# A graph layer on one core: SyncE fetches two sets of 128 edges row by row in chunks away from the stores of packs, and one beside them

## The chip, the core and the metric

The kernel runs on one core of a Trainium2 chip. A core has TensorE (PE: matrix products), VectorE (DVE), ScalarE (ACT), GpSimd (POOL) and SyncE (SP); each runs its own queue of instructions in order, and semaphores tie the queues together. SyncE computes nothing here: it issues transfers. ScalarE and SyncE issue transfers whose addresses are written in the instruction or held in a register; POOL issues indirect gathers, for which 128 row numbers lie in memory. The metric is the device time of one execution in microseconds (us), less is better.

## The reference

One layer of a graph network over 50000 nodes with 160 features each and 1650000 directed edges, sorted by their target, every node with an edge to itself among them. For each edge the source's features are combined with the edge's four numbers by five small weight matrices; the results are summed over the edges of each target, passed through two more matrices, and the layer ends with residuals and a norm:

```python
ss, vv = (s[src], v[src])
e0 = sh[:, 0:1]
e1 = sh[:, 1:4]
dot = jnp.einsum('eui,ei->eu', vv, e1)
out0 = C0 * (ss * e0 @ W1 + dot * INV3 @ W2)
...
m_agg = jax.ops.segment_sum(m, dst, num_segments=n)
...
return x + jax.nn.relu(h)
...
x = _layernorm(x + _L0_gnn_ref(x, edge_attr_4, L0_gnn_W1, L0_gnn_W2, L0_gnn_W3, L0_gnn_W4, L0_gnn_W5, L0_gnn_Ws, L0_gnn_Wv, edge_index), axis=-1)
```

Everything between the gather and the relu is linear in the source's features. So the kernel first sums, for each node, the source rows weighted by each of the four edge numbers, and multiplies by the (merged) weights once per node.

## The kernel before

**Sets, groups, pairs, chunks.** The edges come in *sets* of 128. For one set, 128 rows of `x` (640 bytes each) lie on the 128 partitions, and one product on PE sums them: the left operand `ha` holds, for each edge, its four numbers at the column of its target. Twelve sets are a *pair* of groups, the unit `p` of the main loop; ten pairs are a *chunk* of 120 sets, for which the edge list is loaded and turned at once. There are 105 chunks, numbered from 0. `gather` (L465) says where a set's rows come from: as a rule POOL fetches all 128 by one indirect gather into a tile `xg` (L473), of which there are four, each for a pair. PE waits for each set on its semaphore in `group_sums` (L517, the product at L522). Then VectorE turns the sums (L537) and adds them to a ring of node sums (L546), PE multiplies finished blocks by the weights (L841), VectorE forms residual and norm, and SyncE sends the result (L939).

**Fetchers.** Some sets are not gathered by POOL: another engine fetches their 128 rows one at a time, each with a transfer of 640 bytes whose address is in a register. A `Fetcher` does that, one for ScalarE (tiles `xscalar`) and one for SyncE (`xsync`). `spots(s)` says at which places among the 120 of chunk `s` they stand. `list_rows` (L403) has VectorE turn the row numbers of these sets into byte offsets (`held`, `line`, L412 and L413). From these the engine loads 32 offsets at a time into registers (L377) and issues one transfer for each (L381). `begin` and `deal` pace them: the rows of chunk `s` are dealt out evenly over ten pairs, from pair 4 of chunk `s - 1` to pair 4 of chunk `s`, between whatever else the engine issues.

```python
n = self.counts[s % len(self.counts)] if self.first <= s < NSC - 1 else 0
ats = [math.ceil((FBEGIN + per * (i + 1) / n + FWAIT - per) * PG * G) + self.place for i in range(n)]
```

ScalarE fetches three sets and two sets by turns, from chunk 6 on; SyncE one a chunk, at place 104, from chunk 8 on.

**Packs.** From chunk 5 on the kernel reads an edge list that it has compacted itself: edges from a node to itself are taken out and kept apart (`selves`). That is done in eleven *packs* of up to 128 rows of 1185 edges. A pack's steps, on VectorE mostly, are spread over some nine chunks by due times worked out from when its edges are needed (`due`); near their end SyncE writes the pack back by 17 steps of `store` (L734, each up to 16 transfers at L758), and `read` loads the next one (L615 to L619).

**What sets the order.** The order of each engine's queue is the order in which the program writes the instructions: in the main loop (L1021 to L1073), after each of a pair's twelve products, come a piece of node work, the rows of the fetchers that are due, and the pack's steps that are due. SyncE's queue also carries the loads of edges (`r`, `fd`), of nodes (`xt`, `xr`, `sa`), and the results.

Of the kernel before, what the change touches and what calls it, by code (L numbers as in the profile page):

```python
# [46 lines left out]
ET = mybir.EngineType  # L47
# [31 lines left out]
REST = 15  # L79
LEAD = 3  # L80
BY_SCALAR, SCALAR_FIRST = (3, 2), 6
BY_SYNC, SYNC_FIRST = (1,), 8
FBEGIN, FWAIT = 4, 4

def plan(n_nodes, n_edges):
# [24 lines left out]
def tile_gnn_resnorm(ctx: ExitStack, tc: tile.TileContext, x, src, dst, attr, W1, W2, W3, W4, W5, Ws, Wv, out, n_edges):  # L110
# [110 lines left out]
    NSC = math.ceil(NG / SG)  # L221
# [12 lines left out]
    with tc.tile_pool(name="once", bufs=1) as once, tc.tile_pool(name="raw", bufs=2) as rawp, \  # L234
# [23 lines left out]
        per = SG // PG  # L258
# [42 lines left out]
        def cast(loaded):  # L301
            s, at, ri, fi, fd, ef, af = loaded
            if ri is not None:
                ef = rawp.tile([P, 2, NK, W], F32, name="rf")
                fd = rawp.tile([P, 1], F32, name="ff")
                if s:
                    nc.scalar.copy(fd, fi)
                    begun.append(nc.scalar.copy(ef, ri))
                else:
                    begun.append(nc.vector.tensor_copy(ef[:, 0], ri[:, 0]))  # L310
                    soon.append((ef, ri, fd, fi))
            return s, at, fd, ef, af
# [34 lines left out]
                                                        skip_runtime_bounds_check_because="held within bounds")  # L347
            return spot_of.pop(g)

        fetched = {}  # L350

        class Fetcher:

# [3 lines left out]
                self.landed = [tc.alloc_semaphore(f"{pool.name}{i}") for i in range(4 * (max(counts) + 1))]  # L357

            def spots(self, s):
                n = self.counts[s % len(self.counts)] if self.first <= s < NSC - 1 else 0  # L360
                ats = [math.ceil((FBEGIN + per * (i + 1) / n + FWAIT - per) * PG * G) + self.place for i in range(n)]
                assert all(0 <= at < per * PG * G for at in ats)
                return ats
# [422 lines left out]
        def begin_segment(k):  # L786

            ring[k] = ringp.tile([P, ND, TW], F32, name="ring")
            own = own_blocks(k)
            end = min((own[-1][-1] + 1) * P, nblocks * P) - k * S if own else 0  # L790
            nc.vector.memset(ring[k][:, :, end:], 0.0)
# [61 lines left out]
        steps = place(cast(load(0)))  # L853
# [124 lines left out]
        START = 2  # L978
# [14 lines left out]
        packs, due = [], []  # L993
# [7 lines left out]
        reads, packs = [read for read, _ in packs], [steps for _, steps in packs]  # L1001
        packs[0][:0] = [reads[0], None, None, None]
        done, began = 0, START

        begin_segment(0)
        for k in range(1, NSEG):
            p = first_of[k] // PG
# [5 lines left out]
        for b, g in enumerate(last_of):  # L1013
            p = g // PG
# [79 lines left out]
    with tc.tile_pool(name="up", bufs=1) as up, tc.tile_pool(name="us", bufs=2) as us, tc.For_i(0, once_more, 1):  # L1094
# [18 lines left out]
        for s in range(nseg):  # L1113
# [7 lines left out]
            for c in range(CB):  # L1121
# [3 lines left out]
                at = us.tile([PB, 2, SEG], F32, name="at")  # L1125
# [18 lines left out]
    with tc.tile_pool(name="edges2", bufs=2) as ep, tc.tile_pool(name="ops2", bufs=2) as op, \  # L1144
            tc.tile_pool(name="node2", bufs=1) as np_, tc.tile_pool(name="psA2", bufs=2, space=PSUM) as psA, \
            tc.tile_pool(name="psF2", bufs=1, space=PSUM) as psF:
        with tc.For_i(0, blocks, 1) as b:
# [35 lines left out]
            for h in range(2):  # L1183
# [3 lines left out]
                at = np_.tile([D // 2, NK, NBLK], F32, name=f"ac{h}")  # L1187
# [3 lines left out]
            i = 0  # L1191
# [44 lines left out]
```

## Time and profile before

| what | value |
|---|---|
| median of 3 runs | 15331.41 us (15308.89 to 15333.12) |
| the profiled execution's own time | 15340.96 us |
| its span, from the first to the last instruction | 15339.1 us |
| granted clock of TensorE, mean | 0.583 |
| sets gathered by POOL | 12181 |
| sets fetched by ScalarE, by SyncE | 245 (31360 rows), 96 (12288 rows) |

Rows of the profile name the line, the engine and the operation, the tile written and the ones read, a count, and then times: in groups of instructions the busy us, the mean ns of one, and after the bar the idle time of the engine just before them with what ended it. `PEld` is the load of PE's left operand; `SPq` and `ACTq` are transfers issued by SyncE and ScalarE; a releaser called "issue" means that the engine waited for nothing the profile shows. PE shows two records for a product in 32-bit floats.

### The profile page before, as it was taken

The numbers are of one execution on the slowest core, as the hardware profiler recorded it, in microseconds if no ns is written. First come the engines' busy times: TensorE is split into PE (matmuls) and PEld (weight loads), VectorE is DVE, ScalarE is ACT, GpSimd is POOL, SyncE is SP. The second block draws the span as 40 slices with busy tenths as digits, with TensorE's granted clock in tenths as the row PEclk, the third lists the DMA queues.
The fourth block names the chain that finished last, engine by engine and source line by source line (L and its number), as shares of the span: only waits on it lengthen the run. The fifth ranks groups of instructions, "written<-read, shape, count | busy, mean of one in ns | idle before, by whom it ended". The sixth has DMA issues, their size and how long they took to land. (4 is left out here: it accounts for less than half of the span.)

```text
span 15339.1 us, 182899 instructions
## 1 busy us (share of the span) xinstructions
PE 9998.2 (65%) x28971; PEld 6683.8 (44%) x28972; DVE 7656.0 (50%) x12665; ACT 171.7 (1%) x273; POOL 11588.2 (76%) x12194
## 2 busy tenths in 40 slices
PE   3666566666666666666666666666666666666666
PEld 3444344444444444444444444444444444444444
DVE  8455365445635543563465355445634553554333
ACT  0000000000000000000000000000000000000000
POOL 7777777777777777777777777777777777777777
PEclk6555655555556555555555555555555555655555
DMA  3333333333333333333333333333333333333333
GB/s 82 99 82 93 90 84 86 96 90 83 92 90 87 84 95 91 82 86 95 91 83 92 89 87 84 96 90 82 86 98 89 81 88 88 87 86 86 85 82 74
DMA packets 916668, 1347.44 MB, mean 88 GB/s; under 512 B 296782, under 2 KB 691138, under 8 KB 912806
## 3 DMA queue, kind: packets, MB, share of 16 engines
q0 software_dynamic: 584688, 998.65, 28.1%
q1 hardware_dynamic: 266794, 315.98, 6.7%
q10 hardware_dynamic: 63984, 21.08, 0.8%
q14 instruction: 971, 7.95, 0.2%
q8 instruction: 231, 3.78, 0.1%
HBM read 1263.28 MB, written 71.42 MB: 87 GB/s over the span
## 5 line engine op out<-in xcount | busy, mean ns | idle before, releaser
L473 POOL DMA_INDIRECT xg<-in_x,si x12181 | 11584.7, 951 | 3722.2 <-issue 3591.6
L522 PE MATMUL ps<-xg,ha 128*128 128x160 f32 x24362 | 9236.8, 496 | 5305.4 <-DMA xg<-in_x,si 4585.4
L522 PEld LDWEIGHTS ps<-xg,ha 128*128 128x128 f32 x24362 | 5688.8, 289 | 8616.2 <-DMA xg<-in_x,si 7920.1
L537 DVE STREAM_TRANSPOSE sums<-ps 128x320 f32<-128x320 f32 x1044 | 535.1, 513 | 6130.6 <-PE ps L522 6089.1
L497 DVE TENSOR_TENSOR ha<-hot,pk 128x1536 f32<-128x1536 f32 x1044 | 1830.3, 1753 | 35.9
L841 PE MATMUL phb<-BWk,ring 128*128 128x160 f32 (+1 forms) x3910 | 1250.5, 417 | 0.0
L841 PEld LDWEIGHTS phb<-BWk,ring 128*128 128x128 f32 (+1 forms) x3910 | 1023.7, 295 | 0.0
L546 DVE TENSOR_TENSOR ring<-ring,sums 128x160 f32 x2087 | 684.3, 328 | 325.1 <-issue 190.1
L494 DVE TENSOR_TENSOR hot<-bank,rel 128x384 f32<-128x384 f32 x1044 | 573.1, 549 | 11.2 <-DMA xt<-in_x 9.4
L707 DVE COPY_PREDICATED prow<-marks,prow 128x2370 f32<-128x2370 int32 (+5 forms) x198 | 548.7, 2771 | 1.1
L832 DVE STREAM_TRANSPOSE ring<-xr 128x1280 f32<-128x1280 f32 x188 | 467.8, 2488 | 6.5
L707 DVE COPY_PREDICATED pra<-marks,pra 128x1580 f32<-128x1580 int32 (+5 forms) x198 | 377.0, 1904 | 0.0
L828 DVE TENSOR_TENSOR xr<-xr,bank 128x1280 f32<-128x1280 f32 x188 | 278.9, 1483 | 6.8 <-DVE bank L827 0.5
L186 DVE SCALAR_TENSOR_TENSOR y<-phb,xt 128x320 f32<-128x320 f32 x196 | 95.5, 487 | 296.7 <-PE phb L841 296.2
L826 DVE TENSOR_TENSOR sa<-sa,bank 128x32 f32<-128x32 f32 x188 | 29.7, 158 | 381.7 <-DMA sa<-selves 381.7
L196 ACT ACTIVATE rstd<-mv,eps_t 128x2 f32<-128x2 f32 x196 | 58.0, 296 | 13960.1 <-DVE mv L191 7936.4
L522 PE MATMUL ps<-xscalar,ha 128*128 128x160 f32 x490 | 168.8, 445 | 0.0
L543 DVE TENSOR_TENSOR ring<-ring 128x196 f32<-128x196 f32 (+20 forms) x485 | 149.1, 373 | 1.8
L644 DVE TENSOR_TENSOR hit<-marks,prow 128x395 f32<-128x395 f32 (+1 forms) x33 | 28.0, 847 | 242.4 <-ACT marks L643 242.4
L522 PEld LDWEIGHTS ps<-xscalar,ha 128*128 128x128 f32 x490 | 137.2, 314 | 0.0
L202 DVE TENSOR_SCALAR o<-y,mv,rstd 128x160 f32<-128x160 f32 x391 | 132.3, 380 | 7.5
L704 DVE COPY_PREDICATED_SCALAR hit<-marks,none 128x395 int32 (+5 forms) x198 | 129.7, 655 | 7.0
(352 smaller groups left out, 2369.6 us busy)
## 6 DMA issues: line engine op xcount, KB each, us to landing
xscalar<-in_x ACTq DMA_DIRECT2D x31360, 0.6 KB
xsync<-in_x SPq DMA_DIRECT2D x12288, 0.6 KB
xg<-in_x,si POOLq DMA_INDIRECT x12181
xr<-in_x SPq DMA_DIRECT2D x187, 640.0 KB
r<-edges SPq DMA_DIRECT2D x100, 384.0 KB
edges<-prow SPq DMA_DIRECT2D x1330, 27.8 KB
xt<-in_x SPq DMA_DIRECT2D x195, 160.0 KB
out<-o SPq DMA_DIRECT2D x195, 160.0 KB
```

The lines of the kernel that those rows point to most:

```text
L202: nc.vector.tensor_scalar(o[:n, i], y[:n, i], mv[:n, i, 0:1], rstd[:n, i:i + 1], op0=ALU.subtract, op1=ALU.mult)
L473: part = nc.gpsimd.indirect_dma_start(out=xg[:, j, :], out_offset=None, in_=x, in_offset=bass.IndirectOffsetOnAxis(ap=placed[0][:, u + j:u ...
L494: idle[:] = [nc.vector.tensor_tensor(hot[:, :n], slotsP[:, 0:W].unsqueeze(1).to_broadcast([P, n, W]), rel[:, u:u + n].unsqueeze(2).to_broa ...
L497: nc.vector.tensor_tensor(ha[:, :n], hot[:, :n].unsqueeze(2).to_broadcast([P, n, NK, W]), pk[:, :, u:u + n].rearrange("p k u -> p u k").un ...
L522: mm = nc.tensor.matmul(ps[:, j // G, :], ha[:, j].rearrange("p k w -> p (k w)"), xr, start=j % G == 0, stop=j % G == G - 1)
L537: nc.vector.transpose(at[:, :ng], ps[:, :ng].rearrange("p g (b f) -> p g b f", f=FB))
L543: nc.vector.tensor_tensor(ring[k][:, b, :past], ring[k][:, b, :past], ring[k - 1][:, b, S:S + past], op=ALU.add)
L546: nc.vector.tensor_tensor(here, here, at[:, i], op=ALU.add)
L707: nc.vector.copy_predicated(what[:n, a:e], mi[:, r].unsqueeze(2).to_broadcast([n, e - a, what.shape[2]]), what[:n, a + d:e + d])
L828: nc.vector.tensor_tensor(xr[:, :nq], xr[:, :nq], sumP[:, :nq].unsqueeze(2).to_broadcast([P, nq, D]), op=ALU.mult)
L832: nc.vector.transpose(ring[k][:, :, c0:c0 + nq * W].rearrange("p b (w q) -> p q b w", q=nq), xr[:, :nq].rearrange("p q (b f) -> p q b f", ...
L841: wrote("misc", nc.tensor.matmul(ph[:nb], ring[k][:, i, c0:c0 + nb], BWk[:, i, :], start=i == 0, stop=i == ND - 1))
```

## The change

SyncE's fetcher gets two counts, two and one. Which one holds in a chunk is no longer its number's turn but a question: does a store of a pack stand within the ten pairs in which the chunk's rows are dealt out, or in the ten before? If so, one set, else two. For that the places of all stores are worked out ahead of the main loop, from the packs' steps and due times. The fetcher also gets one more tile (three rather than two) and twelve semaphores rather than eight, since both are sized by the larger count; `line` and `held` become one place wider. ScalarE's fetcher is as before.

```diff
-BY_SYNC, SYNC_FIRST = (1,), 8
+BY_SYNC, SYNC_FIRST = (2, 1), 8
...
-        fetched = {}
+        fetched, stores = {}, []
+
+        def storing(s):
+
+            p = (s - 1) * per + FBEGIN
+            return any(p - per <= at < p + per for at in stores)
...
             def spots(self, s):
-                n = self.counts[s % len(self.counts)] if self.first <= s < NSC - 1 else 0
+                turn = s if self.et != ET.SP else storing(s)
+                n = self.counts[int(turn) % len(self.counts)] if self.first <= s < NSC - 1 else 0
...
+        for steps, a, b in zip(packs, [START] + due, due):
+            stores += [a + (i + 1) / len(steps) * max(1, b - a) for i, step in enumerate(steps)
+                       if isinstance(step, partial) and step.func.__name__ == "store"]
```

Lines after the change are numbered 6 higher from the fetcher on (9 from the main loop on). Of the 96 chunks from number 8 to 103, 56 get two sets and 40 one, in stretches: 8 and 9 two, 10 to 13 one, 14 to 18 two, 19 to 22 one, and so on to 100 to 103 with two.

On PE, in chunk 35 (one with two sets), places 29 to 61 before:

```order
L522 MATMUL ps<-xg,ha 128x160 x9
L522 MATMUL ps<-xscalar,ha 128x160
L522 MATMUL ps<-xg,ha 128x160 x22
L841 MATMUL phb<-BWk,ring 128x160
L522 MATMUL ps<-xg,ha 128x160
```

and now:

```order
L528 MATMUL ps<-xg,ha 128x160 x9
L528 MATMUL ps<-xscalar,ha 128x160
L528 MATMUL ps<-xg,ha 128x160 x5
L528 MATMUL ps<-xsync,ha 128x160
L528 MATMUL ps<-xg,ha 128x160 x16
L847 MATMUL phb<-BWk,ring 128x160
```

The set at place 44 is read from `xsync` instead of `xg`; POOL's queue, in which gathers stand one behind the other with nothing between them, is one gather shorter there.

On SyncE, the rows for the same chunk from their beginning, before:

```order
L939 DMA out<-o 128x2x160
L377 TENSOR_LOAD line
L381 DMA xsync<-in_x 1x640 x26
L784 DMA xt<-in_x 128x2x160
L381 DMA xsync<-in_x 1x640 x6
L377 TENSOR_LOAD line
L381 DMA xsync<-in_x 1x640 x7
L277 DMA fd<-edges 128x1x1
L271 DMA r_60944<-edges 128x4x192
L381 DMA xsync<-in_x 1x640 x25
L377 TENSOR_LOAD line
```

and now:

```order
L945 DMA out<-o 128x2x160
L383 TENSOR_LOAD line
L387 DMA xsync<-in_x 1x640 x32
L383 TENSOR_LOAD line
L387 DMA xsync<-in_x 1x640 x20
L790 DMA xt<-in_x 128x2x160
L387 DMA xsync<-in_x 1x640 x12
L383 TENSOR_LOAD line
L387 DMA xsync<-in_x 1x640 x13
L277 DMA fd<-edges 128x1x1
L271 DMA r_66883<-edges 128x4x192
L387 DMA xsync<-in_x 1x640 x19
```

Ahead of the load of `xt` (node rows) now stand 52 rows instead of 26, and ahead of `fd` and `r` (the edges of a later chunk) 77 instead of 39; the queue's other transfers are the same, in the same order.

## The prediction

> **What bounds the kernel now.** I read the page's totals, then the groups of instructions by line, then the chain of waits at its end. The totals and the two groups that matter (busy, mean ns of one | idle just before them, what ended it):
>
> ```profile
> span 15339.1 us, 182899 instructions
> PE 9998.2 (65%) x28971; PEld 6683.8 (44%) x28972; DVE 7656.0 (50%) x12665; ACT 171.7 (1%) x273; POOL 11588.2 (76%) x12194
> q0 software_dynamic: 584688, 998.65, 28.1%
> q1 hardware_dynamic: 266794, 315.98, 6.7%
> q10 hardware_dynamic: 63984, 21.08, 0.8%
> L473 POOL DMA_INDIRECT xg<-in_x,si x12181 | 11584.7, 951 | 3722.2 <-issue 3591.6
> L522 PE MATMUL ps<-xg,ha 128*128 128x160 f32 x24362 | 9236.8, 496 | 5305.4 <-DMA xg<-in_x,si 4585.4
> ```
>
> POOL is shown at 76%, but its gathers and the idle time just before them add up to 11584.7 + 3722.2 = 15306.9 us of the 15339.1, and 3591.6 of that idle time ended with nothing but the next issue: 0.3 us between one gather and the next, every time. So POOL is a conveyor: 15306.9 / 12181 = 1.2566 us for one set of 128 edges, from end to end. PE waits for those gathers (4585.4 us), and nothing holds POOL. The chain of waits (start, us, what) says so too: gathers back to back, then a tail of less than 30 us.
>
> ```profile
> 15305.09 0.95 POOL xg L473
> 15306.04 0.30 issue
> 15306.34 0.94 POOL xg L473
> ...
> 15310.10 4.83 DMA xg<-in_x,si
> 15314.97 0.90 PE ps L522 x2
> ```
>
> Hence a set that POOL doesn't gather is worth its 1.26 us, if whoever brings it instead is in time and does not slow the rest.
>
> **The change, part by part.**
>
> *Sets off POOL.* The order gives POOL 12125 gathers instead of 12181, and SyncE 152 sets instead of 96: 56 of the 96 chunks from number 8 on get a second set, at place 44 of 120, and 40 keep one. The removed ones lie between chunk 8 and chunk 103, so I take the price there (from 1100 to 15300 us):
>
> ```profile
> L473 POOL DMA_INDIRECT xg<-in_x,si x11306 | 10747.7, 951 | 3452.9 <-issue 3334.4 <-PE ps L522 109.4 <-PE phb L841 5.8
> ```
>
> (10747.7 + 3452.9) / 11306 = 1.2560 us. 56 x 1.2560 = 70.3 us less on POOL. The head and the tail stay.
>
> *Does row traffic slow the gathers that remain?* The trace has stretches of the same length without and with rows: no engine fetches rows from 100 to 880 us but for the last 63 us of it; from 5000 to 5780 us ScalarE and SyncE fetch all the time. POOL's group in the one and in the other:
>
> ```profile
> L473 POOL DMA_INDIRECT xg<-in_x,si x622 | 591.4, 951 | 189.7 <-issue 183.6 <-PE ps L522 6.1
> L473 POOL DMA_INDIRECT xg<-in_x,si x622 | 591.3, 951 | 189.9 <-issue 183.5 <-PE ps L522 6.1 <-DVE st L190 0.3
> ```
>
> The same 622 gathers, 781.1 and 781.2 us. Some 3.5 sets of rows a chunk cost POOL 0.1 us in 780; a gather more or less in that stretch (1.26 us, 2 ns for each) is the most that the comparison could hide, which over 12125 gathers is 24 us either way. I take zero, as the two sums are nearest to it, and keep 24 us for the range.
>
> *SyncE's time.* What one set costs SyncE: 128 rows and four loads of 32 places. The rows of the issuing instructions and loads (count: ns least/median/most), the same for ScalarE, and then two stretches of SyncE's timeline (start us, us):
>
> ```profile
> L381 SPq DMA_DIRECT2D xsync<-in_x x12288: 224/228/9658, 1114.7 to 15118.4; - x199
> L377 SPq TENSOR_LOAD <-line x384: 2110/2225/2553, 1112.5 to 15105.5; - x192
> L381 ACTq DMA_DIRECT2D xscalar<-in_x x31360: 227/228/1279, 817.2 to 15146.2; - x200
> ```
>
> ```profile
> 5066.32 8.32 SPq L381 DMA_DIRECT2D xsync<-in_x  x26
> ...
> 5156.21 0.60 SPq L817 DMA_DIRECT2D xr<-in_x  x1
> 5156.86 0.54 SPq L817 DMA_DIRECT2D sa<-selves  x1
> 5157.44 0.54 SPq L817 DMA_DIRECT2D xr<-in_x  x1
> 5158.02 7.96 SPq L817 DMA_DIRECT2D sa<-selves  x1
> ```
>
> 26 rows in 8.32 us are 0.32 us each, 128 make 41.0 us; four loads at 2.2 make 8.9; so 49.9 us a set. A chunk of 120 sets, 2.5 of them by ScalarE and one by SyncE, lasts 116.5 x 1.256 = 146.3 us. Two sets are 99.8 us. The other work in a chunk without stores is the four lines above (9.6 us) and a few issues of about 0.5 us each: some 12 us. With two sets POOL has 115.5 gathers left in such a chunk, 145.1 us; SyncE's 112 are 77% of it. SyncE holds that for rows at the same price elsewhere: 31360 rows by ScalarE are 245 sets, 2.5 a chunk and three in every other one.
>
> The Trainium skill, "DMA: Bandwidth & Descriptors", Rules for kernel authors, speaks against 128 transfers of 640 bytes: it says to coalesce, since below 64 KB one pays mostly overhead, and gives a fixed cost of about 2 us for one (Anatomy of one DMA). As an estimate from that figure, paid one after the other, two sets would take 256 x 2 = 512 us of a 146 us chunk and the kernel would lose 56 x 366 us, some 20 ms; by 0.32 us they fit. The row decides: the fixed cost is not paid by the issuer.
>
> *Whether the second set is in time.* Its rows are dealt out over five pairs of groups, from pair 4 of the chunk before, and its last row stands 4.67 pairs (68 us) ahead of its matmul in the order; the second set's rows then fill the other five pairs. The trace shows how far SyncE is ahead in a chunk without stores. One set that began at 5066 us (above) ended with these 20 rows, and PE used it here:
>
> ```profile
> 5169.50 13.74 SPq L381 DMA_DIRECT2D xsync<-in_x  x20
> ...
> 5292.12 0.74 PE L522 MATMUL ps<-xsync,ha 128*128 128x160 f32 x2
> ```
>
> 5292.1 - 5183.2 = 109 us early. With twice the rows the last one comes up to 50 us later, and still some 60 us early. What is queued behind the new rows on SyncE (stores of `out` at L939, loads of `xt`, `r`, `xr`, `sa`) shifts by at most that much too, and mostly not at all, because SyncE idles ahead of those: it waited for VectorE's result before L939 for 2679.8 us. ScalarE's queue is not touched.
>
> ```profile
> SPq L939 <- DVE o L202: 2679.8, 104, 86.9
> DVE sa L826 <- DMA sa<-selves: 381.7, 27, 43.5
> PE ps L522 <- DMA xsync<-in_x: 14.1, 4, 7.6
> PE ps L522 <- DVE ha L497: 575.8, 59, 45.6
> ```
>
> The lines on `sa` and `xsync` are the harm that SyncE does when it is late: VectorE waited 381.7 us for shares, PE 14.1 us for a set. These fall where the stores of packs fill the queue, and there the number stays at one.
>
> *If the cover is gone.* POOL runs ahead of PE by up to four tiles. Around 10100 us PE stood for 34.6 us on VectorE, and POOL went on through it, 44 gathers from 10085 to 10140 us; then PE did 24 sets in 8.52 us, 0.36 us each against POOL's 1.26:
>
> ```profile
> 10122.65 8.52 PE L522 MATMUL ps<-xg,ha 128*128 128x160 f32 x48 [34.60 <-DVE ha L497]
> L473 POOL DMA_INDIRECT xg<-in_x,si x44 | 41.8, 951 | 13.4 <-issue 13.1 <-PE ps L522 0.3
> ```
>
> So a lone late set costs nothing below some 35 us.
>
> *VectorE.* One more conversion of 128x32 for each added set, and a wider product:
>
> ```profile
> L412 DVE TENSOR_SCALAR held<-r x341: 166/180/368, 814.2 to 15023.2; 128x32 f32<-128x32 f32 x171
> ```
>
> 56 x 0.180 = 10.1 us on an engine that is 50% busy and whose stalls of up to 45.6 us don't reach POOL. I cost it at nothing; were it to hold POOL each time for its whole length, 10 us.
>
> *Sum.* 15339.1 - 70.3 = 15268.8 us of span. The profiled execution's own time is 15340.96, 1.9 us above its span, so 15270.7. It is 9.6 us above the median of the runs (15331.41). Against that median: 15331.4 - 70.3 = 15261.1 us, 0.46% less.
>
> **Rivals.**
>
> 1. *SyncE becomes the bound (slower).* In the 56 chunks with two sets PE would wait at place 44 in each. It needs SyncE's other work in a chunk to be over 145.1 - 99.8 = 45 us rather than the 12 counted. At 50 us a chunk would last 149.8 instead of 146.3: 56 x 3.5 = +196 us, 15527 us. It decides from 46.5 us of other work on, where the chunk lasts its 146.3 again. For it: `sa` alone took 7.96 us to issue, and one issue of a row took up to 9.66. Against it: it needs the counted 12 us four times over, and stretches with stores, where that happens, are left out. 0.04.
>
> 2. *The 16 DMA engines set the pace (no change).* If a gather's 1.2566 us were the time that its bytes take, the same bytes through another queue would win nothing: 15331 us. Against it: the three queues together keep the engines 28.1 + 6.7 + 0.8 = 35.6% busy, and the next gather is issued 0.3 us after the last, without waiting for it to land. The Trainium skill, "DMA: Bandwidth & Descriptors", Issuing engines are not separate DMA queues, is the rule for this rival: all queues run on the same 16 engines, and issuing from several saves only the sequencer's time, which it calls usually small. Here that issuing time is the whole kernel. 0.03.
>
> 3. *Contention (slower or a smaller gain).* If the added rows lengthen each remaining gather by more than 70.3 / 12125 = 5.8 ns, the change loses; at 2 ns, the most that the two stretches could hide, 15285 us. 0.03, a third of it each for a smaller gain, no change and a loss.
>
> 4. *Some late sets (smaller gain).* In the first double chunk after each of the eleven packs' stores, SyncE may still be behind; 2 us lost in each would leave 15283 us. 0.05.
>
> **How the numbers follow.** The forecast has 0.85; it, rival 4 and a third of rival 3 are faster by over 0.2% (30.7 us, about what a measurement of this kernel tells from no change): 0.91. Rival 2 and a third of 3: 0.04. Rival 1 and a third of 3: 0.05. The range runs from the lowest run less the gain (15308.89 - 70.3 = 15238.6) to the profiled execution's 15270.7 plus the 20 us of rival 3 or 4: 15238 to 15290. It leaves out rivals 1 and 2.
>
> **What the profile after would show.** The group of gathers at 12125, still 951 ns with 0.3 us ahead of each, and a span shorter by 56 of these; 304 matmul records on `xsync` instead of 192; 608 loads of `line` on SyncE; PE's wait for `xsync` still some 15 us, all in chunks with stores. Wrong would be: POOL's waits for PE far above 118 us, PE's waits for `xsync` over some 35 us at a time, or a pitch of gathers above 1.26 us.

## The result and the profile after

The changed kernel takes 15300.47 us (median of 13 runs, 15270.83 to 15303.11), the kernel before, beside it, 15336.82 us (median of 13): a ratio of 0.9976, with a 95% interval from 0.9967 to 0.9984. That is 36.4 us less (25 to 51 by the interval), half of the 70.3 us forecast; the time lies above the range, which ended at 15290 us.

The profile alone would have said otherwise. Its totals, the group of POOL's gathers and what POOL waited for (us in all, times, longest):

```profile
span 15269.1 us, 197459 instructions
L479 POOL DMA_INDIRECT xg<-in_x,si x12125 | 11500.1, 948 | 3735.8 <-issue 3588.8
POOL xg L479 <- PE ps L528: 132.6, 320, 17.3
```

The span is shorter by 70.0 us, as forecast, but two effects that the forecast did not have cancel in it. A gather's mean is 948.46 ns (11500.1 / 12125) instead of 951.05 (11584.7 / 12181), which over 12125 gathers is 31 us less; and POOL, which the trace of before never showed waiting for PE by more than 1.6 us, now waited up to 17.3 us. The first is a matter of the single execution that was profiled (below: the kernel before, profiled again, has 948 too): the profiled execution of the changed kernel is the lowest of its 13 runs, at 15270.83, and the other twelve lie between 15294 and 15303.

So the question is POOL's waits. Its timeline has three of them that the first profile of the kernel before lacks (start, us, what; in brackets the idle time just before and what ended it):

```profile
1876.13 0.94 POOL L479 DMA_INDIRECT xg<-in_x,si  x1 [14.97 <-PE ps L528]
...
7310.52 0.94 POOL L479 DMA_INDIRECT xg<-in_x,si  x1 [3.60 <-PE ps L528]
...
10103.49 0.94 POOL L479 DMA_INDIRECT xg<-in_x,si  x1 [17.31 <-PE ps L528]
```

Together 35.9 us, against 0.3 us of idle time that any gather has: 35.0 us lost. 70.3 - 35.0 = 35.3 us, and the runs show 36.4. The three lie in chunks 12, 49 and 68, at the end of the stores of a pack or just behind it, in chunks that keep one set. The waits of PE, VectorE and SyncE tell who was late:

```profile
PE ps L528 <- DVE ha L503: 843.1, 80, 58.7
PE ps L528 <- DMA xsync<-in_x: 56.9, 5, 27.3
DVE sa L832 <- DMA sa<-selves: 561.5, 34, 66.6
SPq L945 <- DVE o L202: 983.4, 45, 86.5
```

VectorE's wait for the shares `sa`, which SyncE loads, went from 381.7 us (longest 43.5) to 561.5 (longest 66.6); PE's wait for VectorE behind it from 575.8 to 843.1. SyncE's own idle time ahead of the stores of `out` fell, by its row, from 2679.8 us to 983.4: that idle time was its lead.

Where the lead goes is seen at the pack whose stores run through chunks 66 to 68. The first store, the place at which PE reads SyncE's set 104 of chunk 66, and, at the end of the stores, the first load of `xr` (`sa` is loaded 0.7 us behind it); before and after, where PE's wait is added:

```profile
9719.19 0.30 SPq L758 DMA_DIRECT2D edges<-prow  x1
...
9833.12 0.74 PE L522 MATMUL ps<-xsync,ha 128*128 128x160 f32 x2
...
10083.42 0.62 SPq L817 DMA_DIRECT2D xr<-in_x  x1
```

```profile
9699.26 0.31 SPq L764 DMA_DIRECT2D edges<-prow  x1
...
9785.33 0.74 PE L528 MATMUL ps<-xsync,ha 128*128 128x160 f32 x2
...
10065.82 0.63 SPq L823 DMA_DIRECT2D xr<-in_x  x1
...
10098.01 8.46 PE L528 MATMUL ps<-xg,ha 128*128 128x160 f32 x48 [58.67 <-DVE ha L503]
```

Before, SyncE began the stores 113.9 us ahead of that product; after, 86.1 us. The rows of chunk 66, dealt out just ahead of the stores, are two sets now, and so SyncE came 28 us later. From the first store to the load of `xr` it took 364.2 us before and 366.6 after: it won nothing back, and the loads of `xr` and `sa` came as much later. The wait of VectorE at that place grew from 37.0 to 66.6 us, and PE's from 34.60 to 58.67.

The same reading gives 112.3 and 83.4 us at the pack of chunks 47 to 49, 29 us less. At the first pack, whose wait is the second longest, it gives 82.9 and 77.3: only 5.6 us less, while the way from the first store to the loads took 417.6 us rather than 411.1. PE waited 45.55 us there before already, and POOL 1.56 us right behind it:

```profile
1864.34 4.07 PE L522 MATMUL ps<-xg,ha 128*128 128x160 f32 x14 [45.55 <-DVE ha L497]
...
1870.59 0.96 POOL L473 DMA_INDIRECT xg<-in_x,si  x1 [1.56 <-PE ps L522]
```

What of the first pack's 14.97 us comes from rows ahead of the stores is open (see "Which rows" below).

### The profile page after: what moved, and what is told of

It is laid out like the page before. It is cut to its first block, busy times and chain, and to the rows that moved or that the text cites. A ratio compares the mean times of both kernels' runs of the same rounds, so it can differ in the third digit from the quotient of the medians.

```text
span 15269.1 us, 197459 instructions
## 1 busy us (share of the span) xinstructions
PE 9851.5 (65%) x28971; PEld 6664.4 (44%) x28972; DVE 7658.8 (50%) x12721; ACT 171.5 (1%) x273; POOL 11503.6 (75%) x12138
## 5 line engine op out<-in xcount | busy, mean ns | idle before, releaser
L479 POOL DMA_INDIRECT xg<-in_x,si x12125 | 11500.1, 948 | 3735.8 <-issue 3588.8
L528 PE MATMUL ps<-xg,ha 128*128 128x160 f32 x24250 | 9049.2, 492 | 5338.9 <-DMA xg<-in_x,si 4312.8
L503 DVE TENSOR_TENSOR ha<-hot,pk 128x1536 f32<-128x1536 f32 x1044 | 1830.1, 1753 | 35.8
L832 DVE TENSOR_TENSOR sa<-sa,bank 128x32 f32<-128x32 f32 x188 | 29.7, 158 | 561.5 <-DMA sa<-selves 561.5
```

What stands on the lines that cost most here:

```text
L479: part = nc.gpsimd.indirect_dma_start(out=xg[:, j, :], out_offset=None, in_=x, in_offset=bass.IndirectOffsetOnAxis(ap=placed[0][:, u + j:u ...
L503: nc.vector.tensor_tensor(ha[:, :n], hot[:, :n].unsqueeze(2).to_broadcast([P, n, NK, W]), pk[:, :, u:u + n].rearrange("p k u -> p u k").un ...
L528: mm = nc.tensor.matmul(ps[:, j // G, :], ha[:, j].rearrange("p k w -> p (k w)"), xr, start=j % G == 0, stop=j % G == G - 1)
```

## Experiments

Theory A is the account just given: rows *ahead* of the stores take SyncE's lead, and at the end of the stores PE stands longer than POOL's four tiles cover. Theory B: a set taken off POOL is worth only half of what was reckoned. Theory C: rows in flight make every gather longer. Each kernel was timed beside the kernel before on its chip.

**What the sets are worth, without rows.** SyncE fetches one set a chunk as before; the 56 sets are left out.

```diff
-BY_SYNC, SYNC_FIRST = (2, 1), 8
+BY_SYNC, SYNC_FIRST = (1,), 8
...
+            if u <= 44 < u + n and SYNC_FIRST <= s < NSC - 1 and not storing(s):
+                rows[44 - u] = spare, None, 0, None
...
-                mm.wait_op(sem, count, "sem-ge")
+                if sem is not None:
+                    mm.wait_op(sem, count, "sem-ge")
...
```

> SyncE fetches one set a chunk as before; POOL leaves out the 56 sets at place 44 and PE multiplies a tile of zeros there, so those edges are missing from the sums. Theory A and a theory C (rows in flight lengthen every gather by some 3 ns): the whole 56 x 1.256 = 70.3 us less than before, pitch of gathers unchanged, no long wait of POOL. Theory B: 36 us less.

Measured: 15242.09 us against 15307.30, ratio 0.9958 (0.9944 to 0.9972), 65.2 us less; POOL's longest wait for PE 2.8 us. That is the forecast's term within its interval, and B's 36 is not. C is not told apart by it.

**The rows, without what they save.** SyncE fetches as in the changed kernel, POOL gathers all.

```diff
+            if u <= 44 < u + n and (s, 44) in fetched:
+                second[:] = [44 - u, fetched.pop((s, 44))]
...
+                if twice and j == twice[0]:
+                    more_xr, more_sem, more_count, more_key = twice[1]
+                    mm = nc.tensor.matmul(ps[:, j // G, :], ha[:, j].rearrange("p k w -> p (k w)"), more_xr,
+                                          start=False, stop=False)
...
```

> SyncE's rows as in the changed kernel, but POOL gathers those 56 sets too and PE adds them a second time, so they count twice. Theory A: POOL waits for PE some 35 us more than before, in two to four places, all at the end of a pack's stores, and the time is 25 to 45 us above before. Theory C: also some 35 us above before, but by a longer pitch everywhere, 1.259 us instead of 1.256. Theory B: the same time as before.

Measured: 15335.53 us against 15307.30, ratio 1.0018 (1.0009 to 1.0027), 28.2 us more. The group and the two long waits:

```profile
L482 POOL DMA_INDIRECT xg<-in_x,si x12181 | 11553.7, 948 | 3746.3 <-issue 3605.8 <-PE ps L540 122.8 <-PE phb L859 7.0
...
1876.22 0.95 POOL L482 DMA_INDIRECT xg<-in_x,si  x1 [12.01 <-PE ps L540]
...
10142.60 0.94 POOL L482 DMA_INDIRECT xg<-in_x,si  x1 [16.60 <-PE ps L540]
```

12.01 + 16.60 - 2 x 0.3 = 28.0 us, which is the whole of the 28.2. Without these waits the pitch of gathers is (11553.7 + 3746.3 - 28.0) / 12181 = 1.2537 us, and the kernel before, profiled again at the same mean of a gather (948 ns, below), has (11550.4 + 3721.2) / 12181 = 1.2537. So C is out: the rows cost nothing but these two waits.

**Which rows.** The changed kernel leaves the second set out in chunks whose rows fall beside a store or just behind one. Three kernels move that border; `p` is the pair at which a chunk's rows begin.

First, the chunk ahead of the stores is left out as well, 46 sets instead of 56:

```diff
-            return any(p - per <= at < p + per for at in stores)
+            return any(p - per <= at < p + 2 * per for at in stores)
```

> SyncE's second set is also left out in a chunk whose rows are dealt out in the ten pairs just ahead of a store: 46 sets more than before instead of 56. Theory A (the changed kernel loses some 35 us because SyncE enters the stores of a pack with less lead, and at their end the loads of xr and sa and a set of rows are so late that PE stands longer than POOL's four tiles cover): no wait of POOL for PE above 2 us in or behind the stores, and 46 x 1.256 = 57.8 us less than before, some 22 us less than the changed kernel. Theory B (a set off POOL is worth only half of 1.256 us, whatever SyncE does): 46 x 0.65 = 30 us less than before.

Measured: 15254.04 us against 15307.30, ratio 0.9966 (0.9954 to 0.9978), 53.3 us less; that is 17 us more gain than the changed kernel's 36.4, with ten sets fewer. One long wait is left, in the first pack:

```profile
1872.46 0.94 POOL L479 DMA_INDIRECT xg<-in_x,si  x1 [10.12 <-PE ps L528]
```

The others are gone. I had expected none. The rows ahead of the stores are not what makes the difference here: SyncE's queue is the same in the next kernel up to 1884 us, and that one waited no more than 0.9 us at this place. The runs of this kernel lie in two groups, three at 15250 us and three from 15257 to 15261, as they would if such a wait came in some executions and not in others. What decides that is not shown.

Second, the same 56 sets, moved from ahead of the stores to behind them:

```diff
-            return any(p - per <= at < p + per for at in stores)
+            return any(p <= at < p + 2 * per for at in stores)
```

> The ten pairs that are looked at beside a chunk's own window lie behind it rather than ahead of it: one set in the chunk ahead of a store, two in the chunk that follows the stores. 56 more sets than before, as in the changed kernel. Theory A: lead at the entry is what counts, so no wait of POOL for PE above 2 us, and 70 us less than before, 34 less than the changed kernel; should the set at place 44 behind the stores be late, some 5 to 20 us of that go. Theory B and C: 36 us less than before, as the changed kernel.

Measured: 15239.57 us against 15307.30, ratio 0.9957 (0.9943 to 0.9970), 67.7 us less.

```profile
L479 POOL DMA_INDIRECT xg<-in_x,si x12125 | 11503.3, 949 | 3702.0 <-issue 3591.7 <-PE ps L528 93.7 <-PE phb L847 6.1
POOL xg L479 <- PE ps L528: 93.7, 305, 0.9
DVE sa L832 <- DMA sa<-selves: 542.8, 42, 43.9
```

The number of sets, rows and gathers is the changed kernel's; only their place differs, and no wait of POOL for PE is longer than 0.9 us. VectorE's waits for `sa` are as long in sum (542.8 us), but the longest is 43.9 us rather than 66.6, and PE's longest wait for VectorE 46.3 rather than 58.7: it is the longest that counts, not the sum.

Third, two sets on both sides, 66 in all, beside the changed kernel run once more:

```diff
-            return any(p - per <= at < p + per for at in stores)
+            return any(p <= at < p + per for at in stores)
```

> The changed kernel once more, beside the next three on one chip. All theories: 36 us less than before, and with the group of POOL's gathers at the mean of this chip (948 or 951 ns) three long waits of POOL for PE at the end of packs' stores, some 35 us together, so that 70.3 less 35 is what is left.

> Two sets in every chunk whose own ten pairs have no store, ahead of the stores as in the changed kernel and behind them too: 66 more sets than before. Theory A (only the rows ahead of the stores hurt): 66 x 1.256 = 82.9 us less work of POOL and the same long waits of some 35 us, so 48 us less than before. A rival D (rows beside the stores hurt on either side, by the number of them): the waits grow by a quarter or more and the time is the changed kernel's 36 us below before or worse.

Measured: the changed kernel 15271.60 us against 15307.41, ratio 0.9977 (0.9968 to 0.9986), 35.8 us less, with long waits of 16.9 us at most; with 66 sets 15272.61 us, ratio 0.9976 (0.9967 to 0.9985), 34.8 us less. Ten more sets off POOL brought nothing.

```profile
POOL xg L479 <- PE ps L528: 124.7, 267, 20.2
DVE sa L832 <- DMA sa<-selves: 779.7, 54, 73.3
```

VectorE waited 73.3 us at the worst, not 66. A's 48 us were not reached: the two medians lie 1.0 us apart where A has 12.6, so rows behind one pack's stores are not free when there are rows ahead of the next as well. Rival D has the time right; its growth of the waits by a quarter is not in this profile, whose three long waits cost 43.3 us against 37.3 in that of the changed kernel beside it. What the added rows hold up stays open: SyncE began the stores of chunk 66 as late as in the changed kernel (85.9 us ahead of PE's product, against 86.4).

**What holds PE at the end of the stores.** The changed kernel with the loads of `xr` and `sa` two pairs earlier in SyncE's queue:

```diff
-            after_pair(p - 5, ask_own, k, bs, got)
+            after_pair(p - 7, ask_own, k, bs, got)
```

> The changed kernel with xr and sa asked for two pairs earlier in the order (7 instead of 5 ahead of their use), some 29 us of PE's pace. Theory A, with PE standing on VectorE for the shares as the wait that holds POOL: VectorE's waits for sa fall from 561 us to some 250 or less, POOL's long waits go but for a remnant below 10 us, and the time is 60 to 70 us below before. Rival E (it is the late set of rows at place 104 that holds PE): the waits of PE for xsync and POOL's long waits stay, 36 us below before.

Measured: 15236.58 us against 15307.41, ratio 0.9954 (0.9940 to 0.9967), 70.8 us less: all of the forecast's gain.

```profile
POOL xg L479 <- PE ps L528: 88.1, 289, 0.3
PE ps L528 <- DVE ha L503: 505.1, 65, 32.8
PE ps L528 <- DMA xsync<-in_x: 136.9, 7, 31.1
DVE sa L832 <- DMA sa<-selves: 205.1, 19, 35.1
```

The shares were it. PE now waits for late sets of rows longer than in the changed kernel (136.9 us rather than 56.9, up to 31.1 at a time), and not one of these waits reaches POOL: rival E is out.

With the 66 sets and the earlier loads together:

> Both edits: 66 more sets than before and the earlier asking. Theory A: 75 to 83 us below before, as no long wait of POOL is left. Rival E or D: at most 48 us below before.

Measured: 15227.91 us against 15307.41, ratio 0.9948 (0.9934 to 0.9961), 79.5 us less: the fastest version here, ahead of both kernels. One wait of POOL of 6.7 us is left, right behind a wait of PE of 46.1 us for a late set of SyncE's rows: with the shares in time, these sets are the next to be late.

**The cover.** The changed kernel with three tiles for POOL's gathers:

```diff
-            tc.tile_pool(name="idx", bufs=2) as idxp, tc.tile_pool(name="rows", bufs=4) as rowp, \
+            tc.tile_pool(name="idx", bufs=2) as idxp, tc.tile_pool(name="rows", bufs=3) as rowp, \
...
-            t = begun_tiles[0] % 4
+            t = begun_tiles[0] % 3
```

> The changed kernel with three tiles for POOL's gathers instead of four, 12 sets or some 15 us less cover. Theory A: each of the three long waits of POOL grows by 12 to 15 us, and waits of 1 to 13 us appear where the cover was nearly used up, at the end of other packs' stores: 55 to 70 us more than the changed kernel, 20 to 35 us above before. Rival (POOL is never held by the tiles, the long waits have another cause): the same time as the changed kernel.

Measured: 15347.76 us against 15341.10 on this chip, ratio 1.0006 (0.9997 to 1.0015): 6.7 us more than before (by the interval not told from none) where the changed kernel has 36 less, so the tile is worth some 43 us.

```profile
1876.15 0.95 POOL L479 DMA_INDIRECT xg<-in_x,si  x1 [25.39 <-PE ps L528]
...
4519.89 1.03 POOL L479 DMA_INDIRECT xg<-in_x,si  x1 [10.44 <-PE ps L528]
...
7345.77 0.95 POOL L479 DMA_INDIRECT xg<-in_x,si  x1 [13.08 <-PE ps L528]
...
10154.58 0.95 POOL L479 DMA_INDIRECT xg<-in_x,si  x1 [29.95 <-PE ps L528]
```

The three waits grew by 10.4, 9.5 and 12.6 us, and one of 10.44 came: 78.9 us in all where the changed kernel has 35.9, which is 43.0 more, as the runs say. The rival is out. The size was put 12 to 27 us too high, since a wait grew by 10 to 13 us rather than by 12 to 15, and fewer new ones came. A fifth tile wasn't tried.

The cover itself can be read off the profiles, as PE's wait for VectorE less POOL's wait right behind it: 41 to 46 us in the profiles with four tiles (45.55 and 1.56 in the kernel before; 46.89 and 3.60, 57.20 and 14.97, 58.67 and 17.31 in the changed one), 27 to 32 us with three (57.3 and 29.95).

**The mean of a gather.** The kernel before, profiled again:

> The kernel before once more, for a profile on the same chip as the changed kernel's second one. If the mean of a gather is a matter of the chip, POOL's gathers are at 948 or 949 ns here rather than 951, with no wait of POOL for PE above 3 us behind the first 100 us, and the span is some 36 us above the changed kernel's on this chip, 15308. If it is the change that shortens a gather, the mean is 951 ns.

Its time is that of the kernel before, 15341.93 against 15341.10 us (1.0001, 0.9992 to 1.0010), but the profiled execution took 15305.94:

```profile
L473 POOL DMA_INDIRECT xg<-in_x,si x12181 | 11550.4, 948 | 3721.2 <-issue 3583.0 <-PE ps L522 124.4 <-PE phb L841 5.2
```

```profile
L479 POOL DMA_INDIRECT xg<-in_x,si x12125 | 11530.7, 951 | 3782.6 <-issue 3595.5 <-PE ps L528 170.3 <-PE phb L847 6.4
```

The first row is this kernel's, the second that of the three tiles, on the same chip. So 948 ns is not the change's doing, and it isn't a matter of the chip alone, as I had thought.

## Why the prediction was wrong, point by point

- *What bounds the kernel*: right. POOL issues gathers end to end, and what it was spared came off the time, within the intervals: 65.2 us with the sets left out, 70.8 with the loads asked for earlier, 70.3 forecast.
- *Row traffic costs the remaining gathers nothing*: right. With all rows and all gathers the whole loss is two waits at two places.
- *SyncE's time of 49.9 us a set, and the second set early enough in its own chunk*: right as far as the runs show; PE's late sets (14.1 us of waiting before, 56.9 after) all lie in chunks 11, 30, 49, 78 and 88, where stores are.
- *"What is queued behind the new rows on SyncE ... shifts by at most that much too, and mostly not at all, because SyncE idles ahead of those"*: here it failed. This delay of other transfers stood in the sum at nothing, and it cost 35.0 us. The sum of 2679.8 us of idle time was taken as room to spare in each place. It is lead, and in the chunk ahead of the stores the lead was needed: SyncE wins nothing back from their first to their last, so the 28 us taken at the entry were still missing at the end of them, over two chunks later. The prediction asked whether the new rows would be late, and not whom they made late. (That is shown for the packs at chunks 49 and 68; at the first one the rows took 5.6 us of lead.)
- *"... and there the number stays at one"*: that was taken to exclude those chunks, and all three long waits were in them.
- *"So a lone late set costs nothing below some 35 us"*: true as it stands, as the cover measured 41 to 46 us; but it was not held against the waits that were there already. PE's wait of 45.6 us and VectorE's of 43.5 were quoted, and both lie at the end of the first pack's stores, where POOL's 1.56 us shows the cover used up. *VectorE* says of the same waits that they "don't reach POOL": this one just did. With SyncE later the longest were 58.7 and 66.6.
- *Rivals*: number 4 (some late sets) was the nearest. It had them in the chunk behind the stores, at 2 us in each of eleven packs; they were at the end of the stores, at 35 us together in three of eleven, and came through the shares rather than the sets. That term was sized at 22 us in all and measured 35, and it had 5% of the chance.
- *The signs of being wrong*: none of the three showed it. POOL's waits for PE were 132.6 us in sum, little above the 118, since the short ones became fewer (320 instead of 384); PE's longest wait for `xsync` was 27.3 us; the pitch was (11500.1 + 3735.8) / 12125 = 1.2566 us. The longest wait of POOL, 17.3 us instead of 1.6, would have been the sign.
- *The median*: the three runs shown of before gave 15331.41, thirteen gave 15336.82. That is 5 us, and it wasn't what failed: 15336.8 - 70.3 + 35.0 = 15301.5, and the runs show 15300.47.

## What to carry to other kernels

Work given to an engine that idles is paid for out of that engine's lead, and lead is spent where the engine is next the late one. So look at the waits in the stretch *behind* the work you add, not only beside it, and ask how much of the buffers' cover the longest wait there uses already: one longest wait decides, the sum of waits does not. If something queued further on is on the path, move that forward; here one number (7 for 5) gave back the whole loss.

## What was not expected of the hardware

The mean time of an indirect gather took one of two values for a whole execution: 948.2 to 948.7 ns in ten profiles (median 946) and 951 in two (median 949). The kernel before showed 951 in one profile (15340.96 us) and 948 in another (15305.94 us), 35 us apart, as much as the effect measured here. TensorE's granted clock is 0.583 in both. The chip has a part in it: on two chips all 36 executions of the kernel before took 15301.51 to 15314.42 us, on a third 30 of 31 took 15335.20 to 15347.84, and the one of 15305.94 is the 31st. What sets the value stays open. By these 35 us a single execution of each kernel could have given a difference of anything from about 1 to 71 us; the two first profiles gave 70.1 (15340.96 - 15270.83).
